# One VectorE pass for mask and row maximum, and steps that a planner may put on either of two engines

## The chip, the cores and the metric

The kernel runs on one core of a Trainium2 chip. The metric is the device time of one execution in microseconds (us). A core has TensorE (PE: matmuls, and PEld for the loading of their weights), VectorE (DVE), ScalarE (ACT), GpSimd (POOL) and SyncE (SP, which issues most transfers here). Matmul results go to PSUM, which has eight banks of 128 x 512 f32; DVE and ACT read PSUM in this kernel, POOL doesn't.

## What is computed

16 examples of 256 rows with 128 features pass six residual blocks, all in f32. Cut to what matters:

```python
x = x + 0.5 * L0_ffn(layernorm(x))     # gated: silu * linear, two hidden 512x512 layers with gelu
x = x + L0_attn(layernorm(x))          # non-local attention without a softmax
x = x + 0.5 * L0_ffn(layernorm(x))
x = x + 0.5 * L1_ffn(layernorm(x))     # top-2 of 8 low-rank experts, chosen by the first row
x = x + L1_attn(layernorm(x))          # 16 heads of 8, rotary positions, causal
x = x + 0.5 * L1_ffn(layernorm(x))
# inside L1_attn:
scores = jnp.einsum('bhqd,bhkd->bhqk', q, k) * scale
scores = jnp.where(causal, scores, -jnp.inf)
out = jnp.einsum('bhqk,bhkd->bhqd', softmax(scores, axis=-1), v)
```

## The kernel before, in words

The examples are worked in nine groups: seven of two examples (512 rows, "wide") and two of one (256 rows, "narrow"). Each group passes a first feed-forward with the non-local attention behind it, and a second feed-forward with experts, attention and experts behind it. x stays in SBUF throughout.

**The order is planned while the program is written.** Each piece of work is a generator whose steps (`step`, line 228) name an engine, an assumed duration in us, what they need, and the buffers and PSUM banks that they take or drop. A loop at the end of `macaron_kernel` keeps an assumed clock for each engine, asks `begin` (927) when each waiting step could start, and lets `issue` (975) write the earliest. Within an engine that order is the program's; at run time the engines only wait for data. `dve`, `act` and `pool` (237 to 243) give the durations. `find` (914) hands out PSUM banks: the attention's scores take banks 0 to 3 together, and a step with one bank may borrow one of those if `LOAN` us of waiting are saved. The feed-forwards are the main line, with all other lines fitted in. When the main line has ended, `awake` (962) issues products of the identity (`ident` times `ident`) into expected gaps of PE, 0.7 of each gap; the text calls them fillers.

**Feed-forward** (`ffn`, 329): w1T and w2T products, `silu` on ACT, the product on DVE, then two hidden layers in which seven block products replace eight. `sums` (360) makes for each layer four differences T of blocks of h, the first on DVE, the other three on POOL. `left` (384) copies one product to h on ACT. The w3s products end the feed-forward.

**Layernorm** (`normed`, 265): bn_stats and bn_aggr on DVE; four small operations on POOL give rstd and shift; then one ACT operation per 128 rows writes xn. `by_feature` (280) transposes xn on PE and copies it from PSUM to xnT on DVE.

**Attention** (`attention`, 652): `rotary` (633) makes keys and queries, with a last addition on POOL; `keys` (678) writes four masked copies of the keys, on ACT; `queries` (688) two of the queries (qz), on DVE. `maxima` (711) computes scores once to find each row's maximum: for each half t of an example's rows, PE writes scores of 4 x 2 heads x w keys (w is 256 for t=1, 128 for t=0), DVE adds the causal mask `causal` to the diagonal part in PSUM, and one reduction gives the negated maxima of eight heads, into tile mx. `queries_with` (747) transposes mx and adds it to the queries by `mrow`, so that the scores which `weighted` (767) computes again have their maximum subtracted already. There ACT takes the exponential (pr), POOL zeroes the upper triangle, PE multiplies by the values. In the last two groups (`late`) maxima goes by halves of the heads.

The core of the maxima, for each t and each list of pairs:

```python
for n in range(len(pairs)):
    yield dve(8 * P)
    d = sc[:, :, 2 * n : 2 * n + 2, t * P : w]
    nc.vector.tensor_tensor(d, d, causal...to_broadcast([P, 4, 2, P]), ALU.add)
...
for n, v in enumerate(pairs):
    yield dve(8 * w, drop=...)
    nc.vector.tensor_reduce(to[:, :, 1 - v], sc[:, :, 2 * n : 2 * n + 2, :], AX.X, ALU.max, negate=True)
```

All engine instructions go through a helper at line 220, so that the profile shows nearly every one as L220; they are told apart by engine, operation and tile. The tile pb is the whole of PSUM.

Of the kernel before, what the change touches and what calls it, by code (L numbers as in the profile page):

```python
# [12 lines left out]
F32 = mybir.dt.float32  # L13
# [6 lines left out]
P = 128  # L20
# [6 lines left out]
LANDING = 2.2  # L27
LOAN = 2.0
PATIENCE = 2.0
# [20 lines left out]
NEG = -1e30  # L50
# [4 lines left out]
def macaron_kernel(ctx: ExitStack, tc: tile.TileContext, a: dict, out: bass.AP):  # L55
# [63 lines left out]

    causal = cst.tile([P, P], F32, name="causal")  # L120
    ones = cst.tile([1, P], F32, name="ones")
    pht = cst.tile([P, D], F32, name="pht")
# [69 lines left out]
    def constants():  # L192

        yield step("POOL", 1.4, needs=(("in", 0, 0),))
        nc.gpsimd.memset(causal, 0.0)
        nc.gpsimd.affine_select(
            out=causal, in_=causal, compare_op=ALU.is_ge, fill=NEG, base=0, pattern=[[-1, P]], channel_multiplier=1
        )
        nc.gpsimd.memset(ones, 1.0)
        yield step(None, 0.0, sets=(("constants",),))  # L200

        for b in store_of["vm"]:
            yield step("POOL", 1.8)
            nc.gpsimd.memset(b.t, 0.0)
            yield step("POOL", 0.6, drop=(b,))
            for j in range(4):
                o = 8 + 16 * (j // 2)
                nc.gpsimd.memset(b.t.rearrange("p t r j c -> p (t r) j c")[:, :, j, o : o + DK], 1.0)
        for b in store_of["mx"]:
            yield step("POOL", 0.3, drop=(b,))  # L210
            nc.gpsimd.memset(b.t, 0.0)
# [15 lines left out]

    def step(engine, us, table=None, banks=0, take=(), drop=(), after=None, needs=(), sets=(), tiles=None, lag=0.0):
        return dict(
            engine=engine, us=us, table=table, banks=banks, take=take, drop=drop, after=after, needs=needs, sets=sets, lag=lag,  # L230
            tiles=tiles,
        )

    def pe(us, **kw):
# [30 lines left out]
    def normed(t0, n, needs=()):  # L265
        yield step("DVE", 0.12 + 0.26 * n, needs=needs)
        st = sml.tile([P, GT, 6], F32, name="st")
        for t in range(n):
            nc.vector.bn_stats(st[:, t, :], x[:, t0 + t, :])
        mv = scales(st, n)  # L270
        yield step("POOL", 1.2 + 0.17 * n)
        rstd, shift = inverse(mv, n)
        (xn,) = yield step("ACT", 0.39 * n, take=("xn",))
        for t in range(n):
            nc.scalar.activation(
                xn.t[:, t, :], x[:, t0 + t, :], AF.Identity, bias=shift[:, t : t + 1], scale=rstd[:, t : t + 1]
            )
        return xn

    def by_feature(n, xn, keep=False):  # L280
        pt, xnT = yield pe(0.11 * n, banks=1, take=("xnT",), drop=() if keep else (xn,))
        v = pt.t.rearrange("p (t n) -> p t n", n=P)
        for t in range(n):
            nc.tensor.transpose(v[:, t, :], xn.t[:, t, :], ident)
        yield dve(n * P, drop=(pt,))
        nc.vector.tensor_copy(xnT.t[:, : n * P], pt.t[:, : n * P])
        return xnT
# [41 lines left out]
    def ffn(which, t0, n):  # L329
# [30 lines left out]
        def sums(l, h, T):  # L360

            for i, e, x, y, needs in (
                (1, "DVE", (0, 1), (0, 0), ()),
                (2, "POOL", (1, 1), 1, ()),
                (3, "POOL", (1, 1), (0, 1), ()),
                (4, "POOL", (1, 0), 2, (("P6", l, me),)),
            ):
                needs += tuple(k for b in (x, y) if type(b) is tuple for k in has(l, *b))
                made = (("T", i, l, me),)
                drop = (T[2],) if i == 4 else ()  # L370
                (T[i],) = yield (
                    dve(N, needs=needs, take=("T",), sets=made, drop=drop) if e == "DVE"
                    else step("POOL", 0.05 + 0.002 * N, needs=needs, take=("T",), sets=made, drop=drop)
                )
                engine = nc.vector if e == "DVE" else nc.gpsimd
                engine.tensor_tensor(
                    T[i].t[:, :, :M], block(h, *x), T[y].t[:, :, :M] if type(y) is int else block(h, *y), ALU.subtract
                )
# [5 lines left out]
        def left(l, a, nh):  # L384

            yield act(N, sets=(("P1", l, me),))
            nc.scalar.copy(block(nh, 1, 1), in_two(a))

# [110 lines left out]
    def nonlocal_attn(t0, n):  # L499
# [4 lines left out]
        def product(us, lhs, rhs, name, drop=()):  # L504
# [3 lines left out]
            for b in range(nb):  # L508
# [4 lines left out]
                else:  # L513
                    nc.tensor.matmul(pp[:, b, :], lhs[:, b, :], rhs, start=True, stop=True)
            yield dve(nb * D, drop=(bk,))
            m = sml.tile([P, 2, D], F32, name=name, bufs=1)
            nc.vector.tensor_copy(m[:, :nb], pp[:, :nb])
            return m
# [74 lines left out]
    def experts(sg):  # L593
        xn = yield from normed(sg.t0, sg.n, (("ffn", 0, (1, sg.t0)), ("ffn", 1, (1, sg.t0)), ("constants",)))
        xnT = yield from by_feature(sg.n, xn)
        if sg.first:
            nb = len(sg.parts)
            yield step("POOL", 0.2 + 0.1 * nb)
            cls = sml.tile([P, 2, P], F32, name="cls", bufs=2)
            nc.gpsimd.tensor_copy(  # L600
                cls[:, :nb],
                xnT.t[:, : sg.n * P].rearrange("p (b s) -> p b s", b=nb)[:, :, 0:1].to_broadcast([P, nb, P]),
            )
            merged["before", sg.g] = yield from gated(nb, cls)
            yield step(None, 0.0, sets=(("before", sg.g),))
        yield from applied(("before", sg.g), sg, xnT)

    def gated_ahead(g, nb, y):
# [15 lines left out]
        for b in range(nb):  # L624
            nc.tensor.matmul(pc[:, b, :], y[:, b, :], ones, start=True, stop=True)
        yield dve(nb * D, drop=(bk,))
        cls = sml.tile([P, 2, P], F32, name="cls", bufs=2)
        nc.vector.tensor_copy(cls[:, :nb], pc[:, :nb])
        merged["after", g] = yield from gated(nb, cls)
# [3 lines left out]
    def rotary(c0, N, xnT, n, rot):  # L633
# [12 lines left out]
        nc.vector.stream_shuffle(rot[:, 1, :N], rot[:, 1, :N], [i ^ 1 for i in range(32)])  # L646
        yield pool(N)
        nc.gpsimd.tensor_tensor(rot[:, 0, :N], rot[:, 0, :N], rot[:, 1, :N], ALU.add)

    kept = {}  # L650

    def attention(sg):
# [25 lines left out]
        def keys():  # L678
# [3 lines left out]
            for j in (0, 2, 1, 3):  # L682
                yield step("ACT", 0.28 + 0.00083 * N, sets=(("km", sg.t0, j),) + ((("kept", g),) if j == 3 and sg.first else ()))
                nc.scalar.activation(
                    km[:, PLANE[j], c0 : c0 + N], kT[:, :N], AF.Identity, bias=kone[:, j : j + 1], scale=kmask[:, j : j + 1]
                )

        def queries():
# [3 lines left out]
            for v in range(2):  # L692
                yield step("DVE", 0.15 + 0.0005 * N, sets=(("qz", sg.t0, v),))
                nc.vector.tensor_scalar(qz[:, v, c0 : c0 + N], qT[:, :N], qmask[:, v : v + 1], None, ALU.mult)
            yield step(None, 0.0, needs=(("km", sg.t0, 3),), drop=(rot,))
# [7 lines left out]
        v0 = sg.parts[0][1][0]  # L703
        yield step("ACT", 0.53 + 0.225 * n, drop=(bk,), sets=(("v", sg.t0),))
        for i in range(2):
            nc.scalar.copy(
                vm.t[:, v0 : v0 + n].rearrange("p t r (i h) c -> p (t r) i h c", i=2)[:, :, i, :, 16 * i : 16 * i + DK],
# [3 lines left out]
        def maxima(i):  # L711
# [5 lines left out]
            def scores(t, pairs):  # L717
# [16 lines left out]
                sc = q.t[:, :, : len(pairs) * 2 * w].rearrange("p r (j k) -> p r j k", k=w)  # L734
                for n in range(len(pairs)):
                    yield dve(8 * P)
                    d = sc[:, :, 2 * n : 2 * n + 2, t * P : w]
                    nc.vector.tensor_tensor(
                        d, d, causal.unsqueeze(1).unsqueeze(1).to_broadcast([P, 4, 2, P]), ALU.add
                    )  # L740

                to = mx[0].t[:, t, :].rearrange("p (r o h c) -> p r h o c", r=4, o=2, h=2)[:, :, :, :, 0]
                for n, v in enumerate(pairs):
                    yield dve(8 * w, drop=(q,) if n == len(pairs) - 1 else ())
                    nc.vector.tensor_reduce(to[:, :, 1 - v], sc[:, :, 2 * n : 2 * n + 2, :], AX.X, ALU.max, negate=True)

# [167 lines left out]
    def find(n, short):  # L914
# [10 lines left out]
        return best.clear, [best], None  # L925

    def begin(line):

# [10 lines left out]
        if n["table"] == "exp" and table[0] != "exp" and not ended[0]:  # L939
            t += PATIENCE  # L940
        return max(t, clock[n["engine"]]) if n["engine"] else t

# [32 lines left out]
    def issue(line):  # L975
# [5 lines left out]
        t = max([t, since] + [s.clear for s in bufs])  # L981
        e, us = n["engine"], n["us"]
        if e:
# [84 lines left out]
def _tables():  # L1068
# [15 lines left out]
    sel = np.stack([RANK * ~second, RANK * second, f % RANK, np.where(second, -0.5, 0.5)], axis=1)  # L1084
    made = {"cosT": cos, "sinT": sin, "qmask": qmask, "kmask": kmask, "kone": kone, "mrow": mrow, "sel": sel}
    return {n: np.ascontiguousarray(v, dtype=np.float32) for n, v in made.items()}
# [55 lines left out]
```

## Time and profile before

| | |
|---|---|
| median of 3 runs | 973.13 us (972.97 to 973.29) |
| profiled execution | 972.04 us |
| its span, first to last instruction | 970.4 us |
| mean granted TensorE clock | 0.996 |
| ACT table loads | 78 |
| DMA | 13.76 MB, mean 14 GB/s |

The span is that of the profiled execution alone, and 1.6 us of its time lie around it. Busy time is the time in which an engine had an instruction under way; instructions that overlap on one engine are not counted twice, so a group's busy time can be less than its count times the mean. In a group's line stand: source line, engine, operation, tile written <- tiles read, shapes, count | busy us, mean ns of one | idle us of the engine just before, and what ended it. A wait's line gives us in total, times, and the longest. The chain of work that ended last goes back from the last instruction, at each step to what released it.

### The profile page before, as it was taken

Reading aid. Unit: us, or ns where it says so; the run is one execution under the profiler, and the core shown is the slowest. Engines: PE = TensorE matmul, PEld = TensorE weight load, DVE = VectorE, ACT = ScalarE, POOL = GpSimd, SP = SyncE. Lnnn points to the kernel's source line nnn. Section 1 sums busy time; section 2 is a strip of 40 time slices with the busy share of each in tenths; the row PEclk is TensorE's granted clock in tenths of the full one; section 3 lists DMA queues with packets and bytes.
Section 4 is the critical chain, followed back from the end, with each engine's and each line's share of the span. In section 5 each row is a group of like instructions: output and inputs, shape, how many; then the busy total and the mean of one; then the engine's idle time right before and its main releaser. Section 6 shows DMA issues by size and latency. Waiting matters only on the chain.

```text
span 970.4 us, 16624 instructions
## 1 busy us (share of the span) xinstructions
PE 918.1 (95%) x6600; PEld 690.0 (71%) x6600; DVE 646.1 (67%) x1470; ACT 450.2 (46%) x672; POOL 371.8 (38%) x572
## 2 busy tenths in 40 slices
PE   6999999999999999999999999999999899898887
PEld 4877878666676767686786667767777777786565
DVE  5654456937687646857569376856577676869673
ACT  2244344365535463553552755254652547472342
POOL 5422334241534225341553425242444135343342
PEclk9999999999999999999999999999999999999999
DMA  7000000000000000000000000000000000000000
GB/s 249 16 1 1 1 12 7 5 1 2 12 23 1 1 1 22 12 1 1 13 22 1 2 12 1 23 1 1 12 12 11 1 12 2 23 7 12 1 22 7
DMA packets 14717, 13.76 MB, mean 14 GB/s; under 512 B 2032, under 2 KB 12080, under 8 KB 14640
## 3 DMA queue, kind: packets, MB, share of 16 engines
q1 hardware_dynamic: 12624, 8.11, 2.8%
q0 software_dynamic: 1600, 4.20, 1.5%
q8 instruction: 52, 0.85, 0.4%
q10 hardware_dynamic: 416, 0.39, 0.1%
q14 instruction: 25, 0.20, 0.1%
HBM read 10.60 MB, written 2.10 MB: 13 GB/s over the span
## 4 chain that ended last, share of the span: by engine, by line
PE 65%; DVE 18%; ACT 7%; issue 4%; POOL 3%; DMA 1%; SPq 1%; DVEq 0%; ACTq 0%; POOLq 0%
PE pb L220 65%; DVE mx L220 4%; DVE h L220 3%; ACT pr L220 3%; DVE pb L220 2%; ACT L220 2%; ACT xn L220 1%; POOL rstd L220 1%; DVE st L220 1%; DVE x L220 1%; DMA w3s<-in_w3T_dram 1%; DVE T L220 1%; ACT sil L220 1%; DVE den L220 1%; DVE gw L220 1%
## 5 line engine op out<-in xcount | busy, mean ns | idle before, releaser
L220 DVE TENSOR_TENSOR h<-h,pb 128x512 f32<-128x512 f32 (+1 forms) x180 | 111.9, 622 | 104.4 <-PE pb L220 98.7
L220 PE MATMUL pb<-T,hS 128*128 128x256 f32 (+1 forms) x576 | 134.5, 366 | 10.7 <-DVE h L220 5.8
L220 ACT ACTIVATE h<-h 128x512 f32<-128x512 f32 (+1 forms) x108 | 62.4, 581 | 173.7 <-DVE h L220 173.6
L220 POOL TENSOR_TENSOR T<-h,T 128x512 f32<-128x512 f32 (+1 forms) x72 | 83.7, 1163 | 122.5 <-DVE T L220 56.8
L220 PE MATMUL pb<-qkv 32*128 32x256 f32 (+2 forms) x1536 | 115.1, 405 | 14.9 <-ACT pr L220 7.6
L220 POOL TENSOR_SCALAR nm<-mv 128x4 f32<-128x4 f32 (+3 forms) x62 | 15.1, 243 | 274.1 <-DVE mv L220 267.4
L220 PEld LDWEIGHTS pb<-T,hS 128*128 128x128 f32 x576 | 95.0, 190 | 33.4 <-issue 8.1
L220 ACT ACTIVATE pr<-pb 128x1536 f32<-128x1536 f32 x64 | 92.4, 1449 | 54.6 <-PE pb L220 47.2
L220 ACT ACT_TABLE_LOAD x77 | 98.8, 1283 | 39.2 <-PE pb L220 36.3
L220 POOL TENSOR_SCALAR_AFFINE_SELECT pr<-pr 128x512 f32<-128x512 f32 x128 | 78.2, 635 | 100.0 <-ACT pr L220 99.7
L220 ACT ACTIVATE xn<-x,shift,rstd 128x128 f32<-128x128 f32 x188 | 77.7, 483 | 79.3 <-POOL shift L220 73.6
L220 DVE TENSOR_REDUCE mx<-pb 128x8 f32<-128x2048 f32 (+1 forms) x64 | 111.8, 1750 | 0.5
L220 DVE TENSOR_TENSOR pb<-pb,causal 128x1024 f32<-128x1024 f32 x64 | 78.5, 1227 | 36.1 <-PE pb L220 33.6
L220 PEld LDWEIGHTS pb<-qkv 32*128 32x128 f32 x1536 | 68.2, 184 | 48.1 <-ACT pr L220 16.0
L220 PE MATMUL pb<-xnT,w1T 128*128 128x512 f32 (+1 forms) x144 | 69.0, 561 | 3.0 <-ACT sil L220 1.5
L220 PE MATMUL pb<-xnT,w2T 128*128 128x512 f32 (+1 forms) x144 | 68.7, 559 | 1.3 <-ACT sil L220 1.0
L220 DVE SCALAR_TENSOR_TENSOR h<-pb,s,sil 128x512 f32<-128x512 f32 (+1 forms) x72 | 48.2, 684 | 31.1 <-ACT sil L220 21.2
L220 PE MATMUL pb<-T,h2T 128*128 128x256 f32 (+1 forms) x288 | 64.8, 362 | 3.3 <-DVE T L220 3.0
L220 PE MATMUL pb<-T,h1T 128*128 128x256 f32 (+1 forms) x288 | 66.3, 360 | 0.6 <-DVE T L220 0.6
L220 DVE TENSOR_TENSOR x<-x,pb 128x256 f32<-128x256 f32 (+2 forms) x79 | 37.4, 474 | 43.0 <-PE pb L220 42.8
L220 PE MATMUL pb<-h,h1T 128*128 128x256 f32 (+1 forms) x288 | 65.3, 364 | 0.2 <-DVE h L220 0.2
L220 PE MATMUL pb<-h,hS 128*128 128x256 f32 (+1 forms) x288 | 65.4, 360 | 0.0
(121 smaller groups left out, 1558.3 us busy)
## 6 DMA issues: line engine op xcount, KB each, us to landing
out_dram<-x SPq DMA_DIRECT2D x7, 256.0 KB, 2.3
x<-in_x_dram SPq DMA_DIRECT2D x6, 256.0 KB, 4.7
h1T<-in_h1T_dram SPq DMA_DIRECT2D x1, 1024.0 KB, 9.3
h2T<-in_h2T_dram SPq DMA_DIRECT2D x1, 1024.0 KB, 10.1
ab<-in_eab_dram,at POOLq DMA_INDIRECT x32, 2.8
x<-in_x_dram SPq DMA_DIRECT2D x3, 128.0 KB, 4.9
w1T<-in_w1T_dram SPq DMA_DIRECT2D x1, 256.0 KB, 3.9
w2T<-in_w2T_dram ACTq DMA_DIRECT2D x1, 256.0 KB, 4.1
```

Source lines behind the costliest of these rows:

```text
L220: return lambda *args, **kw: tc.keep_in_program_order(getattr(self.engine, name)(*args, **kw))
```

## The change

The mask and the row maximum become one DVE operation per head and t: it adds a 128 x w piece of `causal` (now 256 wide, with the diagonal in its right half) to the scores in PSUM and at the same time keeps the maximum in an accumulator, which is written to one column of mx. The maximum isn't negated any more; the table `mrow` is. The step of each two heads becomes two steps of four operations.

`either` makes a step with two possible engines, each with an assumed duration. `pick`, called from `begin` and `issue`, takes the engine whose clock, duration and hop to the next engine would end first. `either` is used for xn (ACT or DVE), the copies xnT, gram, gph, eff, cls and h (DVE or ACT), all four T and rotary's addition (DVE or POOL), one copy for the experts' choice (POOL or DVE), the keys' and queries' masked copies and the copy of the values (ACT or DVE). `LOAN` becomes 1.0. The tile `ones` shrinks to one element that is broadcast.

```diff
-LOAN = 2.0
+LOAN = 1.0
+SPARED = 0.0
...
+    def either(*alt, **kw):
+
+        return step(alt[0][0], alt[0][1], alt=alt, **kw)
...
+    def copied(n, **kw):
+
+        return either(("DVE", 0.07 + 0.00105 * n), ("ACT", 0.16 + 0.00083 * n), **kw)
...
-        (xn,) = yield step("ACT", 0.39 * n, take=("xn",))
+        (xn,) = yield either(("ACT", 0.39 * n), ("DVE", 0.21 * n), take=("xn",))
...
-                (T[i],) = yield (
-                    dve(N, needs=needs, take=("T",), sets=made, drop=drop) if e == "DVE"
-                    else step("POOL", 0.05 + 0.002 * N, needs=needs, take=("T",), sets=made, drop=drop)
+                (T[i],) = yield either(
+                    ("DVE", 0.07 + 0.00105 * N), ("POOL", 0.19 + 0.0021 * N), needs=needs, take=("T",), sets=made, drop=drop
...
-                for n in range(len(pairs)):
-                    yield dve(8 * P)
-                    d = sc[:, :, 2 * n : 2 * n + 2, t * P : w]
-                    nc.vector.tensor_tensor(
-                        d, d, causal.unsqueeze(1).unsqueeze(1).to_broadcast([P, 4, 2, P]), ALU.add
-                    )
...
-                    yield dve(8 * w, drop=(q,) if n == len(pairs) - 1 else ())
-                    nc.vector.tensor_reduce(to[:, :, 1 - v], sc[:, :, 2 * n : 2 * n + 2, :], AX.X, ALU.max, negate=True)
+                    for h in range(2):
+                        yield step("DVE", 4 * (0.1 + 0.00105 * w), drop=(q,) if n == len(pairs) - 1 and h else ())
+                        for r in range(4):
+                            d = sc[:, r, 2 * n + h, :]
+                            nc.vector.tensor_tensor_reduce(
+                                out=d, in0=d, in1=causal[:, 2 * P - w :], scale=1.0, scalar=-3e38, op0=ALU.add, op1=ALU.max,
+                                accum_out=to[:, r, 1 - v, h, 0:1],
+                            )
...
+    def pick(n, t):
+
+        if n["alt"]:
+            n["engine"], n["us"] = min(n["alt"], key=lambda a: max(t, clock[a[0]]) + a[1] + HOP[a[0]] + (SPARED if a[0] == "DVE" else 0.0))
...
-    made = {"cosT": cos, "sinT": sin, "qmask": qmask, "kmask": kmask, "kone": kone, "mrow": mrow, "sel": sel}
+    made = {"cosT": cos, "sinT": sin, "qmask": qmask, "kmask": kmask, "kone": kone, "mrow": -1.0 * mrow, "sel": sel}
```

## The prediction

> **What bounds the kernel now.** I read the page from the top: busy shares, the chain, the costliest groups. Then the waits of TensorE alone, and the busy time by stage.
>
> ```profile
> span 970.4 us, 16624 instructions
> PE 918.1 (95%) x6600; PEld 690.0 (71%) x6600; DVE 646.1 (67%) x1470; ACT 450.2 (46%) x672; POOL 371.8 (38%) x572
> ...
> PE 65%; DVE 18%; ACT 7%; issue 4%; POOL 3%; DMA 1%; SPq 1%; DVEq 0%; ACTq 0%; POOLq 0%
> PE pb L220 65%; DVE mx L220 4%; DVE h L220 3%; ACT pr L220 3%; DVE pb L220 2%; ACT L220 2%; ACT xn L220 1%; POOL rstd L220 1%; DVE st L220 1%; DVE x L220 1%; DMA w3s<-in_w3T_dram 1%; DVE T L220 1%; ACT sil L220 1%; DVE den L220 1%; DVE gw L220 1%
> ```
>
> TensorE is full. The chain's largest item off it is the mask and maximum: mx 4% and pb 2%, some 58 us. By stage (each row: stretch, its length, then busy time of PE, PEld, DVE, ACT, POOL):
>
> ```profile
> 0.00:871.00 871.00, 836.70 (x5729) 629.37 (x5729) 577.50 (x1319) 417.35 (x628) 339.06 (x508) 1.00 0.05 15
> 871.00:971.00 100.00, 81.40 (x873) 60.61 (x871) 68.63 (x151) 32.83 (x45) 32.70 (x64) 0.99 0.04 10
> ```
>
> 871 is where the last feed-forward's w3s products end. Up to there TensorE idles 34.3 us: 8.1 in the first 50, 26.2 after. The last 100 us (the tail) hold 18.6 us of idleness, and 116 fillers, `ident` products that `awake` issues into expected idleness. 13 fillers took 3.17 us in the timeline, 0.244 each, so 28 us of the tail's busy time is no work: 47 of its 100 us are waiting. Between 50 and 870 TensorE waited thus:
>
> ```profile
> PE pb L220 <- DVE h L220: 6.4, 9, 1.5
> PE pb L220 <- DVE T L220: 3.6, 6, 0.9
> PE pb L220 <- ACT sil L220: 3.4, 4, 1.0
> PE pb L220 <- DVE mx L220: 3.4, 6, 0.9
> PE pb L220 <- ACT pr L220: 2.8, 7, 1.1
> PE pb L220 <- POOL T L220: 2.2, 4, 0.9
> ```
>
> So the middle has at most 26 us to give, the tail 47. The matmuls stay the same, fillers apart.
>
> **Part 1: the mask and the maximum.** Now (64 adds, 32 + 32 reductions):
>
> ```profile
> L220 DVE TENSOR_TENSOR pb<-pb,causal 128x1024 f32<-128x1024 f32 x64 | 78.5, 1227 | 36.1 <-PE pb L220 33.6 <-ACT h L220 2.1
> L220 DVE TENSOR_REDUCE mx<-pb 128x8 f32<-128x2048 f32 x32 | 73.1, 2284 | 0.4
> L220 DVE TENSOR_REDUCE mx<-pb 128x8 f32<-128x1024 f32 x32 | 38.7, 1216 | 0.1
> ```
>
> Together 190.3 us of DVE. Instead there are 512 fused passes, half 128 wide, half 256, and the built program shows a second instruction behind each, writing one column of mx: 1024 for 128. The arithmetic per pair of heads falls from 1024 added and 2048 reduced elements to 2048 (t=1), from 1024 and 1024 to 1024 (t=0); the fixed costs rise eightfold. No row shows a fused pass or its read, so bounds. Low: four BATCH_NORM_STATS2 of 128 elements took 0.87 us, one 0.279, so followers come 0.197 apart, 64 ns over 128 elements at the reductions' 1.04 ns (2284-1216 over 1024); passes at 0.197 and 0.330 with the read hidden make 256 x 0.527 = 135 us. High: the full durations of x<-x,pb (0.286 at 128, 0.416 at 256) and a read as long as wt<-mx (0.154): 256 x 1.010 = 259 us. I take the low passes and a read of 0.092, the MATCH_VALUE_LOAD row, since it too is an instruction without a tensor pass in front of which nothing waits: 256 x (0.289 + 0.422) = 182 us, 8 below now. On the chain 58 us x (182/190.3 - 1) = -2.5 us; at the ends -17 and +21.
>
> [...]
>
> **Part 2: steps on either of two engines.** The built order shows that the choice is made. By instructions:
> - xn: 142 of 188 go from ACT (77.7/188 = 0.413 each, -58.7) to DVE (1.12 us for four, 0.28, +39.8). Four in a row take 1.12 instead of 1.65, which the chain meets about six times: 6 x 0.53 x 142/188 = -2.4 us.
> - The differences T: 59 wide and 15 narrow ones from POOL (1.285, 0.73) to DVE (0.684, 0.41): DVE +46.6, POOL -86.8. TensorE's 2.2 us behind POOL T should go: -2.2.
> - rot: 8 + 3 from POOL to DVE, +6.7. Copies of h, vm and keys' masks to DVE: 18, 16, 10, +10.7, about +6, +4.8. cls to DVE +2.
> - To ACT: 28 xnT, 21 of gram, gph, eff and cls, 10 qz: DVE -17.8, -8.2, -5.3; ACT +15.2, +7.2, +7.1. ACT also gets 19 more table loads (97 for 78), 19 x 1.283 = +24.4.
>
> Sums: DVE +85 (with the mask 723, 75% of the span), ACT -25, POOL -101. The table loads I cost at nothing: the moved xn hide them, 58.7 against 24.4. Without that cover: the chain holds 2% (19 us) of table loads out of 98.8, so 24.4 x 0.2 = +4.9. The indirect DMAs' number is the same; on POOL's queue less stands in front of them.
>
> What DVE's load costs: between 50 and 870 TensorE waited for DVE 16.4 us (h, T, mx, and 2.0, 0.6, 0.4 for x, y, xnT) at a DVE share of 66%. If waits go with the inverse of the idle share, 0.34/0.25, that is +5.9. Since a step goes to DVE only where its clock is expected to be free first, I take half, +3.
>
> Added work with two SBUF inputs also meets POOL. At 25.05 us (columns: start, length, operation):
>
> ```profile
> 24.61 1.64 POOL L220 TENSOR_TENSOR T<-h,T 128x512 f32<-128x512 f32 x1 [1.03 <-DVE T L220]
> 26.22 1.71 POOL L220 TENSOR_TENSOR T<-h 128x512 f32<-128x512 f32 x1
> ```
> ```profile
> 25.05 3.43 DVE L220 TENSOR_TENSOR h2T<-h2T,rot 128x512 f32<-128x512 f32 x2
> ```
>
> DVE took 1.75 instead of 0.68 each, POOL 1.64 and 1.71 instead of 1.27. With 85 such T and rot on DVE and POOL busy 28% of the time, 24 meetings x 1.07 = 25 us on DVE, of which 18% (DVE's share of the chain) would be 4.6; the +3 contains what I take of it. [...]
>
> **Part 3: the tail.** LOAN 1.0 and the choices let the planner finish more attention before the last w3s. In the built order, behind that point, transposes of mx fall from 10 to 8 and softmax exponentials from 14 to 11: one example's maxima are out of the tail. In the chain these stood at 877.7 to 893.9, 16.2 us; but some 8 us of matmuls (24 pr, 40 qkv, 4 wo and small ones) come in front of the point instead. -8 net. Fillers give the same from another side: 25 fewer (91 for 116), 25 x 0.244 = 6.1, and as fillers fill 0.7 of an expected gap, 8.7 us less gap. I take -8.7.
>
> **Sum.** -2.5 - 2.4 - 2.2 + 0 + 3 - 8.7 = -12.8. The profiled execution took 972.04 (span 970.4 and 1.6 around it): 959.2. The runs' median, 973.13, is 1.1 higher: **960**, -1.3%.
>
> **Rivals.**
> - *Larger gain* (0.22). The read hides behind the next pass and DVE's relief reaches the middle. For it: followers only 64 ns over their elements. Mask at 135 us: -17 instead of -2.5, so 946; with the +3 gone 943.
> - *DVE full* (slower, 0.20). Passes don't overlap because each read must wait until its pass has drained: 259 us, in the maxima's own steps. DVE then reaches (646+85+69)/970 = 82%; waits for DVE go as 0.34/0.18: 16.4 x 0.89 = +14.6. Chain: +21 - 2.4 - 2.2 + 14.6 - 8.7 = +22: 995. It decides from where a pass of 256 with its read costs over about 0.48 us (0.422 x 207/182; with 207 us in all the chain gains 5 and the waits 8, against -13 from the other terms). For it: 1024 instructions, a planner that counts 0.369 for that pair; against it: BN rows that overlap.
> - *Eaten in the middle* (0.10). The gains stand, 15.8, but table loads (+4.9), meetings with POOL (+4.6) and DVE's load in full (+5.9) take them: -0.4, so 971 to 975.
> - That the choice isn't made is excluded by the built order.
>
> **Chances.** The forecast's case (953 to 969) 0.48. A measurement of this kernel tells about 0.2%, 1.9 us, from no change. The third rival lies across that bound and is split 0.02, 0.06, 0.02. Faster by more: 0.48 + 0.22 + 0.02 = 0.72; within: 0.06; slower: 0.02 + 0.20 = 0.22. The range, 944 to 981, leaves out the far ends of both rivals.
>
> **What will show it.** The pair: fused passes of 256 plus read, spaced 0.42 (0.33 or 0.57 by the ends). The tail after the last w3s near 82 us instead of 100 with 8 more of matmuls before it. PE waits for POOL T gone, for DVE h and mx at most a third up. DVE busy about 723. If TensorE's idle time between 50 and 870 rises beyond 35 us, the sum is wrong in Part 2; if the tail is as long as now, in Part 3; if DVE's mask rows exceed 207 us, in Part 1.

## The result, and the profile after

The change makes no difference that can be measured: 972.66 us (median of 12 runs, 969.52 to 975.53) against 973.05 (12 runs, 971.73 to 973.84), a ratio of 0.9997 [0.9981, 1.0012] (in brackets a 95% interval, here and below). The runs of the changed kernel spread over 6.0 us and those of before over 2.1; the profiled one took 970.75 at a mean granted clock of 0.988, while the five above 973.5 had 0.981 to 0.984. The forecast was 960 and a clear gain. The time came out where the third rival, "eaten in the middle", had put it, but not by that rival's way: the middle gained. The page of the changed kernel, at the places that were shown of before (span, busy times, chain by engine and by line):

```profile
span 969.0 us, 17385 instructions
PE 924.9 (95%) x6550; PEld 696.2 (72%) x6550; DVE 714.0 (74%) x2584; ACT 428.9 (44%) x564; POOL 282.0 (29%) x481
...
PE 76%; DVE 13%; ACT 5%; issue 3%; SPq 1%; POOL 1%; DMA 0%; POOLq 0%; DVEq 0%; ACTq 0%
PE pb L221 76%; DVE pb L221 4%; ACT L221 2%; ACT pr L221 2%; DVE xn L221 1%; DVE h L221 1%; DVE mx L221 1%; DVE rot L221 1%; DVE T L221 1%; ACT h L221 1%; POOL pr L221 1%; SPq L74 1%; DVE qkv L221 0%; ACT sil L221 0%; DVE den L221 0%
```

Two things are to be seen. The chain did what was hoped: TensorE's share of it rose from 65 to 76%, and mx and pb fell from 6 to 5%. And TensorE idles less (44.1 us of the span instead of 52.3), but it is *busy* 6.8 us longer, although 50 products are gone, 25 fillers of two, worth 6.1 us. The same work thus took 12.9 us longer. The mean granted clock is 0.988 instead of 0.996, and 0.8% of 969 us is 8 us, an estimate of what the clock can account for of the 12.9, and about what the shorter waits gave (8.2). It is rather too high, since part of the lower clock lies in the start (0.91 there instead of 0.97), where TensorE was busy for 43.3 us instead of 43.1.

The stages show where. Each is bounded by ends of w3s products, the last of a feed-forward, found in the timeline of either profile (length in us, with TensorE's idle time behind the stroke):

| stage | before | after | difference |
|---|---|---|---|
| start, to the first group's w3s | 51.2 / 8.1 | 57.0 / 13.7 | +5.8 |
| middle, to the 12th feed-forward's | 577.3 / 14.8 | 570.1 / 5.1 | -7.2 |
| to the 17th's | 214.7 / 9.9 | 219.0 / 9.5 | +4.3 |
| last feed-forward | 27.9 / 1.5 | 47.5 / 5.0 | +19.6 |
| tail | 99.3 / 18.0 | 75.4 / 10.8 | -23.9 |

**The start.** The timeline of after (start, length, engine and operation; in brackets the idle time before and who ended it):

```profile
16.53 1.26 POOL L221 TENSOR_TENSOR h1T<-h1T,rot 128x512 f32<-128x512 f32 x1
16.61 6.66 DVE L221 TENSOR_SCALAR xn<-x,rstd,shift 128x128 f32<-128x128 f32 x4 [1.18 <-POOL shift L221]
17.73 1.80 POOL L221 MEMSET vm<- 128x2048 f32 x1
19.50 1.30 POOL L221 TENSOR_TENSOR h1T<-h1T,rot 128x512 f32<-128x512 f32 x1
20.74 3.12 POOL L221 MEMSET vm<- 128x128 f32 x9
```

The second group's four xn, chosen for DVE, take 6.66 us instead of 1.12, as four at 75.12 do with nothing of POOL's beside them; POOL is never free in this stretch, and its own operations keep the lengths that they had before: 1.26 and 1.30 for these two products (1.26 both), 1.80 for the memset of 128x2048 (1.80). TensorE waited for it up to 7.2 us at a time. Before, ACT wrote them in 1.65 beside the same POOL work:

```profile
15.90 1.65 ACT L220 ACTIVATE xn<-x,shift,rstd 128x128 f32<-128x128 f32 x4 [5.54 <-DMA rot<-in_woT_dram]
```

The waits of TensorE over the whole span of after (us, times, longest):

```profile
PE pb L221 <- DVE xn L221: 13.4, 9, 7.2
PE pb L221 <- ACT pr L221: 8.2, 11, 1.7
PE pb L221 <- DVE mx L221: 3.6, 4, 1.4
```

**The end.** The last feed-forward as a whole, first of before, then of after (columns as in the prediction; the third number from the end is the granted clock):

```profile
843.20:871.10 27.90, 26.36 (x254) 22.71 (x254) 18.14 (x46) 18.10 (x28) 10.81 (x20) 1.00 0.02 6
```
```profile
846.10:893.60 47.50, 42.54 (x382) 33.57 (x381) 33.46 (x142) 28.16 (x35) 12.77 (x25) 0.89 0.03 7
```

128 more products, 16.2 us more of busy TensorE and 3.4 more of idleness. The busy time by stretch, two of after, then two of before:

```profile
870.00:880.00 10.00, 7.74 (x47) 5.20 (x40) 9.92 (x58) 0.90 (x3) 1.20 (x4) 0.67 0.00 0
880.00:890.00 10.00, 8.39 (x64) 7.32 (x67) 7.51 (x28) 6.36 (x9) 1.19 (x2) 0.82 0.06 15
```
```profile
870.00:880.00 10.00, 9.75 (x100) 6.72 (x98) 7.13 (x22) 7.62 (x11) 6.60 (x16) 1.00 0.01 2
880.00:890.00 10.00, 7.77 (x73) 6.38 (x72) 9.82 (x20) 1.39 (x5) 1.10 (x1) 1.00 0.05 14
```

In after the last feed-forward is still under way in these 20 us (in before the tail has begun). DVE is busy throughout the first ten, ACT and POOL hardly at all; TensorE idles 2.3 of them, and the granted clock is 0.67 on the mean. Taken finer, it is 1.00 up to 873.37 and then one half for 10.24 us:

```profile
873.37:883.61 10.24, 9.19 (x37) 6.78 (x32) 9.99 (x55) 3.01 (x6) 2.20 (x5) 0.50 0.00 0
```

If half of these 9.19 busy us is due to the clock, that is 4.6 of the 19.6, an estimate. TensorE's timeline of after says how it comes about:

```profile
872.02 3.04 PE L221 MATMUL pb<-qkv 32*128 32x256 f32 x16 [1.30 <-DVE mx L221]
...
878.73 0.76 PE L221 MATMUL pb<-ones,y 1*128 1x128 f32 x2 [0.60 <-DVE x L221]
```

Scores of the next maxima wait for DVE's passes, TensorE's queue stands behind them, and after the wait these 16 products take 3.04 us, the first six of them in pairs 0.38 apart and still at full clock. In the middle of the profile of before such 16 mostly took 0.94.

The kernel before has such a stretch too, the second of its two above: DVE as full, TensorE idle for 2.2 us. But this is in the tail, where fillers run in the gaps, and the clock stays at 1.00:

```profile
882.46 3.17 PE L220 MATMUL pb<-ident 128*128 128x128 f32 x26
```

Up to the end of the main line `awake` issues no filler. That the fillers are what kept the clock up is argued and not shown: no run put any in front of that point, and the tail of `shake_choice` (section 4 of the experiments) had 0.93 on the mean with them.

**The fused pass itself** kept what was forecast. Timeline of after:

```profile
869.38 0.43 DVE L221 CUSTOM_DVE_ANT_0 pb<-pb,causal 128x256 f32<-128x256 f32 x1 [0.80 <-PE pb L221]
869.73 0.14 DVE L221 DVE_READ_ACCUMULATOR2_ANT mx<- 128x1 f32 x1
869.73 0.47 DVE L221 CUSTOM_DVE_ANT_0 pb<-pb,causal 128x256 f32<-128x256 f32 x1
870.11 0.14 DVE L221 DVE_READ_ACCUMULATOR2_ANT mx<- 128x1 f32 x1
...
870.87 0.14 DVE L221 DVE_READ_ACCUMULATOR2_ANT mx<- 128x1 f32 x1
870.87 0.71 DVE L221 STREAM_TRANSPOSE den<-pb 128x512 f32<-128x512 f32 x1
```

A pass of 0.47 and a read of 0.14 repeat every 0.38, not every 0.61: the rows overlap. So a cost taken from the groups' means would be far off. Four of 256 take 1.63 us in all (869.38 to 871.01), four of 128 take 1.09 (877.20 to 878.29): 64 x 2.72 = 174 us for the whole part, where 182 were forecast and 190.3 were there before. The next operation of DVE starts together with the last read, 1.49 us after the first pass (0.96 for four of 128, at 878.16).

### The profile page after: what moved, and what is told of

It reads as the page before. It is cut to its first block, busy times and chain, and to the rows that moved or that the text cites. A ratio compares the mean times of both kernels' runs of the same rounds, so it can differ in the third digit from the quotient of the medians.

```text
span 969.0 us, 17385 instructions
## 1 busy us (share of the span) xinstructions
PE 924.9 (95%) x6550; PEld 696.2 (72%) x6550; DVE 714.0 (74%) x2584; ACT 428.9 (44%) x564; POOL 282.0 (29%) x481
## 4 chain that ended last, share of the span: by engine, by line
PE 76%; DVE 13%; ACT 5%; issue 3%; SPq 1%; POOL 1%; DMA 0%; POOLq 0%; DVEq 0%; ACTq 0%
PE pb L221 76%; DVE pb L221 4%; ACT L221 2%; ACT pr L221 2%; DVE xn L221 1%; DVE h L221 1%; DVE mx L221 1%; DVE rot L221 1%; DVE T L221 1%; ACT h L221 1%; POOL pr L221 1%; SPq L74 1%; DVE qkv L221 0%; ACT sil L221 0%; DVE den L221 0%
## 5 line engine op out<-in xcount | busy, mean ns | idle before, releaser
L221 DVE CUSTOM_DVE_ANT_0 pb<-pb,causal 128x128 f32<-128x128 f32 (+1 forms) x512 | 165.9, 388 | 23.7 <-PE pb L221 23.4
L221 POOL TENSOR_SCALAR_AFFINE_SELECT pr<-pr 128x512 f32<-128x512 f32 x128 | 81.8, 663 | 202.6 <-ACT pr L221 202.5
L221 PE MATMUL pb<-qkv 32*128 32x256 f32 (+2 forms) x1536 | 126.6, 407 | 11.8 <-ACT pr L221 8.2
L221 PEld LDWEIGHTS pb<-T,hS 128*128 128x128 f32 x576 | 98.0, 194 | 24.3 <-issue 8.0
L221 POOL TENSOR_SCALAR nm<-mv 128x4 f32<-128x4 f32 (+3 forms) x62 | 17.6, 285 | 316.2 <-DVE mv L221 314.3
L221 PEld LDWEIGHTS pb<-qkv 32*128 32x128 f32 x1536 | 76.1, 184 | 45.6 <-ACT pr L221 20.3
L221 DVE DVE_READ_ACCUMULATOR2_ANT mx<- 128x1 f32 x512 | 71.7, 140 | 0.0
L221 PE MATMUL pb<-h,h2T 128*128 128x256 f32 (+1 forms) x288 | 65.0, 361 | 0.0
L221 PEld LDWEIGHTS pb<-w3s,h 128*128 128x128 f32 x512 | 60.8, 192 | 4.5 <-issue 2.5
L221 DVE TENSOR_SCALAR xn<-x,rstd,shift 128x128 f32<-128x128 f32 x142 | 52.6, 458 | 15.6 <-POOL shift L221 15.1
```

What stands on the lines that cost most here:

```text
L221: return lambda *args, **kw: tc.keep_in_program_order(getattr(self.engine, name)(*args, **kw))
```

## The experiments

Theories, by the letters that the expectations use. **G**: the middle's gain is given back at the start, where four xn on DVE meet POOL's work, and in the last feed-forward. **P**: fused passes are too dear, as in the rival "DVE full". **Q**: the planner counts fused passes too short (4 x (0.1 + 0.00105 w): 1.48 and 0.94 us, against 1.63 and 1.09 from first start to last end), and so TensorE's queue stands behind waits that the plan doesn't know. **H**: the splitting of a step into halves lets other work in between. **S**: the order that the planner happens on is worth several us either way, whatever the rules. **C**: only steps on either engine make the order depend so much on small differences, so that Part 2's effect is that of an order and not of the engines' relief. All times are medians; the ratio is to the kernel before, in the same session.

**1. One part at a time.** Part 1 alone in the kernel before (`fused_only`):

```diff
-                for n in range(len(pairs)):
-                    yield dve(8 * P)
...
-                    nc.vector.tensor_reduce(to[:, :, 1 - v], sc[:, :, 2 * n : 2 * n + 2, :], AX.X, ALU.max, negate=True)
+                    for h in range(2):
+                        yield step("DVE", 4 * (0.1 + 0.00105 * w), ...)
+                        for r in range(4):
...
+                            nc.vector.tensor_tensor_reduce(
```

> The kernel before with Part 1 alone: fused pass and accumulator read in steps of four, every step on its old engine, LOAN 2.0. Theory G: in the changed kernel four passes of 256 with their reads take 1.63 us, four of 128 about 1.07, so 64 x 2.70 = 173 us against 190 of adds and reductions: same or a little faster, 967 to 973. Theory P: their rows sum to 237.6 us, 47 more than now, and with 58 us of mask and maximum on the chain the time rises by 10 or more, to 983 or above.

969.31 us, 0.9964 [0.9951, 0.9978]. DVE is busy 625.3 us, 20.8 less than before: the passes are cheaper than what they replace, and P falls.

The other half (`choice_only`): the changed kernel with the old add and reduction, and so with `either`, `pick` and LOAN 1.0 alone.

> The changed kernel with Part 1 undone: adds and reductions as before (without the negation, with mrow's sign as changed), their old assumed durations, all choices kept; the planner makes its order anew. Theory G: DVE loses a little, the start and the end remain as in the changed kernel: 972 to 980. Theory P: without the passes' cost the choices show their gain: 958 to 966.

961.55 us, 0.9876 [0.9861, 0.9892]. The start is as bad (xn 6.65 us at 16.28, first w3s end 56.8), and still this half alone is 1.2% faster. Two gains, of 3.7 and 11.5, that together give 0.4: either the parts hurt each other, or each number is partly that of an order. (961.55 is within what P expected of this run, but P had fallen with the run before.)

**2. The start.** The four xn back on ACT, everything else, the plan too, as it was (`xn1_on_act`), or POOL's memsets of vm later (`late_memsets`):

```diff
+        if not normeds:
+            chosen[0] = "ACT"
+        normeds.append(t0)
```
```diff
-            yield step("POOL", 1.8)
+            yield step("POOL", 1.8, needs=(("ffn", 1, (0, 4)),))
```

> The changed kernel with one decision undone by hand: the second group's first xn (four operations) is written on ACT instead of DVE, and the planned order is kept, so nothing else moves. Theory G (the gain of the middle is given back at the start and in the last feed-forward): in the changed kernel these four operations took 6.66 us on DVE while POOL ran its memsets and weight products, and PE came 5.8 us later out of the first group than before; on ACT they take 1.65 us, so the time falls by 5 to 6, to about 967, and the first group's w3s products end near 51.2 as before. Theory P (the fused passes cost too much, and the start is caught up later): the time falls by less than 2, to 971 or more.

969.02 us, 0.9959 [0.9945, 0.9972]. The first w3s end at 52.9 instead of 57.0; a wait for ACT's xn of 4.6 is left, as there was before. 4.1 of the 5.8 us return at the start, and 3.6 of the whole time, where 5 to 6 were expected. TensorE's rows in the profile come in the same order as in the changed kernel, so nothing but these four operations is moved.

> The changed kernel, with POOL's memsets of the two vm tiles held back until the second group's first feed-forward has ended; the planner's order changes from there on. If POOL's work at the same time is what stretched the four xn operations on DVE from 1.1 to 6.66 us, they take 2.5 us or less here (one weight product of POOL still beside them), and the first group's w3s end near 52.5 instead of 57.0; the time falls by some 4, with a few us either way from the new order. If DVE's xn is slow for another reason at that place, they still take over 5 us.

967.42 us, 0.9941 [0.9926, 0.9956]; first w3s end 52.7. The timeline:

```profile
15.82 2.48 POOL L221 TENSOR_TENSOR h1T<-h1T,rot 128x512 f32<-128x512 f32 x2
15.91 3.00 DVE L221 TENSOR_SCALAR xn<-x,rstd,shift 128x128 f32<-128x128 f32 x4 [1.17 <-POOL shift L221]
```

With 2.48 us of POOL's work beside them the four take 3.00, more than expected, since both products now fell beside them. With 7.5 us beside them they took 6.66. G is shown for the start. The single records of the two traces say what holds xn: here the first two each end 0.08 us after one of the products (1.26 and 1.30 long), and the other two, with nothing beside them, take 0.34; in the changed kernel the first and the third end 0.08 us after a memset of 1.80 that followed the product (3.00 and 3.60 long). Both kinds of POOL's work hold them. The later memsets move other work too, so the rest of this gain isn't charged to the start.

**3. The plan's costs and its steps.** Measured costs (`true_costs`), and eight passes in one step at measured cost (`whole_steps`):

```diff
-                        yield step("DVE", 4 * (0.1 + 0.00105 * w), ...)
+                        yield step("DVE", 4 * (0.1325 + 0.00105 * w), ...)
```
```diff
+                    yield step("DVE", 8 * (0.1325 + 0.00105 * w), ...)
                     for h in range(2):
-                        yield step("DVE", 4 * (0.1 + 0.00105 * w), ...)
```

> The changed kernel with the fused steps planned at what they were measured: 1.605 us for four passes of 256 (1.63 measured) and 1.07 for four of 128, instead of 1.475 and 0.938. Theory Q (the planner counts DVE's new steps too short, 64 x 0.26 = 17 us in all, so it fills DVE too far and its order is late at the end): the time falls to 958 to 965, and the last feed-forward no longer takes 47 us. Theory S (the two parts don't disturb each other; the order that the planner happens on is worth several us either way, above all near the end, and the changed kernel met a poor one): any value between 960 and 977, with no tie to the cost.

962.85 us, 0.9902 [0.989, 0.9915]. But the last feed-forward, which Q was to explain, is still 48.7 us long at a clock of 0.89; the gain lies between it and the start (782.8 us instead of 789.1), with 8.2 us of idleness instead of 14.6. The rows of the fused pass speak against Q's ground as well: DVE goes on to its next operation 1.49 and 0.96 us after the first of four passes, which is what the planner counted before (1.48 and 0.94). So this run's costs are too long for the time in which DVE is taken, and its gain isn't explained by truer costs.

> The changed kernel with the fused passes of a pair in one planned step of eight again, at the measured cost (3.21 and 2.14 us), so that nothing is planned between its halves. Theory H (steps cut in halves let other DVE work in between, so that each maximum and the work between both finish later): 958 to 965, and faster than the kernel with halves at the measured cost. Theory Q: like that kernel within 3 us. Theory S: no tie.

969.32 us, 0.9963 [0.995, 0.9976]: 6.5 us slower than halves at the same costs. H finds no support; by C, below, one order is a weak test of it.

Measured costs and the xn on ACT (`true_xn1`):

> The changed kernel with both mends: fused steps planned at their measured length (962.9 alone) and the second group's first xn on ACT with the order kept (3.7 off the changed kernel alone). The order is that of the kernel with the measured lengths, so the start's gain should add to it: 958 to 960. If the later waits take the start's gain up, 962 to 963.

960.26 us, 0.9874 [0.9858, 0.989], 2.6 below `true_costs`, with TensorE's rows in the same order; first w3s end 52.4, the rest of the stages as there to within 0.5 us. The start's cost thus shows a second time in another order.

**4. Other orders of the same kernels.** `SLACK` (line 31; 30 before) is a tie window of the planner: among steps of one engine that could start within it, rank decides. It touches neither what is computed nor any engine's choice by itself.

```diff
-SLACK = 0.05
+SLACK = 0.06
```

0.04, 0.06 and 0.07 were tried, as `shake2_`, `shake_` and `shake3_`, of the kernel before, of Part 1 alone (fused), of the choices alone (choice) and of both (after).

> The changed kernel with the planner's tie window SLACK at 0.06 instead of 0.05: no step's cost or engine rule changes, but the order comes out anew. Theory Q: within 3 us of the changed kernel, 970 to 976, since the costs are still too short. Theory S: it may move by 5 us or more.

> The kernel with the choices and the old adds and reductions (choice_only, 961.55), with SLACK at 0.06 instead of 0.05. Theory Q: within 3 us, 958 to 965. Theory S: it may move by 5 us or more.

> The kernel before with SLACK 0.06 instead of 0.05. Theory S (the order that the planner happens on is worth several us, whatever the rules): it moves by 3 us or more either way. Theory C (only the choice of engines makes the planner so sensitive, because it multiplies the decisions that hang on small differences of the assumed clocks): within 3 us, 970 to 976.

> The kernel before with Part 1 alone (969.3 at SLACK 0.05), at 0.06. Theory S: it moves by 3 us or more. Theory C: within 3 us, 966 to 972. If Part 1 is a gain of its own, it is faster than the kernel before at the same 0.06, by 2 to 6.

> The choices with the old adds and reductions, at SLACK 0.04 (961.6 at 0.05, 980.1 at 0.06). Theory S and theory C both: anywhere between 958 and 982. A value near 962 makes 980 the odd one, a value near 975 makes 962 the lucky one.

> The kernel before at SLACK 0.04 (973.1 at 0.05, 973.6 at 0.06). Theory C (without choices the order is steady): 970 to 976. Theory S: may lie elsewhere.

> Part 1 alone at SLACK 0.04 (969.3 at 0.05, 959.5 at 0.06). If Part 1 by itself is worth the 21 us of DVE that it saves, spread by where it is on the chain, its mean over the three lies 5 to 12 below that of the kernel before: 958 to 972 here. If 959.5 was a lucky order, 968 or more.

> The changed kernel at SLACK 0.04 (972.7 at 0.05, 967.0 at 0.06). If Part 2's choices are worth nothing on the mean once Part 1 is there, its mean over the three lies at or above that of Part 1 alone: 965 to 978 here. If they are worth 5 or more, 950 to 960.

> Part 1 alone at SLACK 0.07, a fourth order of the same rules: 957 to 971 if the mean gain of Part 1 is 5 to 12; 972 or more if the gain was the orders' luck.

> The choices with the old adds and reductions at SLACK 0.07 (971.1 at 0.04, 961.6 at 0.05, 980.1 at 0.06; mean 970.9). If Part 2 is worth little on the mean: anywhere from 960 to 982, the mean of four 968 to 974.

> The changed kernel at SLACK 0.07, a fourth order with both parts. If the choices cost what the start loses (4) and gain about that in the middle, the mean of four lies within 4 of that of Part 1 alone; this one 960 to 976.

Measured, in us (the column 0.05 is from above; ratios of the others below):

| | 0.04 | 0.05 | 0.06 | 0.07 | mean |
|---|---|---|---|---|---|
| before | 972.64 | 973.05 | 973.62 | | 973.1 |
| Part 1 alone | 960.20 | 969.31 | 959.48 | 959.45 | 962.1 |
| choices alone, with LOAN 1.0 | 971.14 | 961.55 | 980.07 | 987.25 | 975.0 |
| both | 969.26 | 972.66 | 966.97 | 979.09 | 972.0 |

Ratios to before: Part 1 alone 0.9871 [0.9854, 0.9887], 0.9867 [0.985, 0.9883], 0.986 [0.9843, 0.9876]; choices alone 0.999 [0.9979, 1.0001], 1.0081 [1.0068, 1.0094], 1.0155 [1.0138, 1.0172]; both 0.9966 [0.9953, 0.9978], 0.9936 [0.9923, 0.9949], 1.006 [1.0042, 1.0078]; before itself 1.0001 [0.9991, 1.001] and 1.0006 [0.9996, 1.0015].

C is shown for choices put into the kernel before: the same windows move that kernel by 1 us, and the choices alone by 26. It isn't shown on top of Part 1, where both parts move by 12 and Part 1 alone by 10. S falls for the kernel before, which it had moving by 3 us or more. Line by line, TensorE's rows in the profiles differ thus from those at 0.05: the kernel before in 7 and 131 lines, Part 1 alone in some 300, at 0.04 and 0.06 only after the first 789 of 1122 rows. With choices they differ from row 120 or so of some 1090 on, in 343 to 837 lines. The likely reason, argued and not shown: a step that goes to the other engine moves two assumed clocks, and with them every later choice. The 1.2% gain of `choice_only` was that of one order. What C doesn't cover: Part 1 alone, for which it had 966 to 972 at 0.06 (959.48 measured), also spreads by 10, since its order at 0.05 is worse behind the 14th feed-forward than the other three (which lie within 0.8 us). The end of the program is sensitive without choices too. Expectations were missed by choices alone at 0.07 (up to 982 expected), by both at 0.07 (up to 976), and by the mean of both, which was to lie within 4 of that of Part 1 alone and lies 9.9 above it.

By stages, means of the profiled executions of those kernels (us):

| | start | middle | to the 17th | last feed-forward + tail | span |
|---|---|---|---|---|---|
| before (3) | 51.5 | 577.3 | 215.0 | 127.4 | 971.2 |
| Part 1 alone (4) | 51.9 | 567.3 | 222.4 | 118.6 | 960.3 |
| choices alone (4) | 56.3 | 571.7 | 220.4 | 123.9 | 972.4 |
| both (4) | 56.1 | 571.7 | 217.4 | 124.8 | 970.0 |

Part 1 gives 10 in the middle and 9 at the end and costs 7 in between. Part of that is work which crossed the bounds: 24 products fewer run in its middle, and 40 to 66 more up to the 17th. Its middle is 567.2 to 567.4 in all four, but these are hardly different orders up to there, so this is one observation rather than four. Choices on top of it cost 4 at the start, 4 in the middle and 6 at the end, and give 5 between. The start's loss (3.7 to 6.0 us against the mean of before) is in all eight kernels with choices. The slowest kernel, choices alone at 0.07, shows the end of after once more, and worse (its last feed-forward ends at 904.9):

```profile
880.00:890.00 10.00, 6.41 (x33) 4.49 (x33) 9.47 (x17) 0.76 (x2) 1.28 (x5) 0.60 0.00 0
890.00:900.00 10.00, 9.43 (x54) 8.53 (x54) 6.51 (x26) 4.58 (x7) 1.77 (x2) 0.54 0.05 15
900.00:910.00 10.00, 8.55 (x111) 6.32 (x109) 2.84 (x10) 7.69 (x8) 4.92 (x10) 1.00 0.01 2
```

DVE is full for 10 us, TensorE idles 3.6 of them, and in the next 10, when it is 94% busy, the clock granted is still 0.54: 54 products in 9.43 us, where 111, not all of the same shapes, take 8.55 afterwards. The clock is at one half from 882.04 to 899.11. This mechanism needs no fused passes: here the old add and reduction run. The mean clock of this kernel is 0.976. It doesn't come with every order: three of the eight kernels with choices have no time at half clock in their last feed-forward.

## Why the prediction was wrong

*Part 1, the passes' cost: right in size, and slightly high.* 182 us forecast, 174 from first start to last end of its steps, 169.5 by DVE's total in Part 1 alone (190.3 - 20.8). The forecast spacing of a pair of 256 was 0.42; it is 0.38, and 0.25 for 128 instead of 0.29. A pass with its read takes about 115 ns more than its elements at the 1.04 ns that the prediction used for one (0.38 - 256 x 0.00104 = 0.114; 0.25 - 128 x 0.00104 = 0.117). The trace has rows of 455 ns for a pass of 256, the read's of 140 not counted, with a spacing of 380, read included; as a price of instructions in a row the rows' own lengths are too high here. "DVE full" falls, on its own condition: 0.38 is below 0.48.

*Part 1, "On the chain 58 us x (182/190.3 - 1) = -2.5 us": mis-sized.* Part 1 alone measured -12.4, -3.7, -14.1 and (against the mean of before) -13.6 in four orders. The ratio scaled the rows of the chain and left out that a DVE relieved of 21 us can come earlier to everything else; the rival of a larger gain, whose term was -17, had that effect in it.

*Part 2, -2.4 - 2.2 + 3: wrong in sign.* The counts were right: DVE 714 (723 forecast), ACT 429 (425), POOL 282 (271). TensorE's waits for POOL's T are gone, as forecast (2.2 us before, none after). In the middle waits fell more than forecast: idleness 14.8 to 5.1, although DVE's load rose, so "+3" was too dear there. It was too cheap at the start: "a step goes to DVE only where its clock is expected to be free first" is true of an assumed clock that knows nothing of POOL's work beside it, and 5.5 us were lost in one place. The prediction priced these meetings for T and rot, operations with two SBUF inputs, and not for xn. It had 25 us on DVE for the first; the wide T there took only some 6 more than at 0.684 each (45 at 0.782, 42 at 0.729). The 142 xn took 52.6 us, where 39.8 were counted. Of the stretched xn two each ended 0.08 us after an instruction of POOL's, beside products (`late_memsets`, 1.26 and 1.30 long) and beside memsets (the changed kernel, 1.80) alike; by what the one engine holds the other no run shows.

*Part 3, "some 8 us of matmuls … come in front of the point instead. -8 net": the step that failed.* The tail became 75.4, even shorter than the 82 forecast, and fillers fell to 91 as forecast. But in front of the point it cost 19.6 us in the last feed-forward and 4.3 before it, not 8: these sum to 23.9, all that the tail gave. The moved work was counted in matmuls at full clock on a TensorE that has nothing to wait for. It came with its maxima, on a DVE that then had no free time for 10 us, in a stage where no filler runs; TensorE waited, and the half clock granted after the wait made its own products longer (the eight `pb<-wo,oT` at 876.05 took 2.08 us; 1.10 in the kernel before at 888.33, at 1.00). That this jam is the reason is read from the profile; no run took the maxima out of that stage in the same order. Over four orders the last feed-forward and the tail together changed by -2.6 (124.8 - 127.4), where the prediction had -8.7 for LOAN and the choices; Part 1 alone changed them by -8.8, and LOAN and the choices on top of it cost 6.

*And the sum as such.* It added terms as if the order were given. With choices it isn't: spreads of 12 and 26 us among equal kernels are as large as the forecast gain, and a range that treats one built order's terms as the change's worth can't be trusted to better than that. The prediction's condition on idleness between 50 and 870, 35 us, wasn't met (it fell to 15.6); the condition on the tail wasn't either. Both looked at stages one by one and missed that work had crossed the point between them.

*What stays open.* Whether longer assumed costs (Q) help on the mean or gave one good order: two kernels share that order. How much of the choices' loss is LOAN 1.0 was not tried. The means of three or four orders are rough: choices alone, +1.9, can't be told from nothing, whereas choices on top of Part 1 lost in all four orders (+9.1, +3.4, +7.5, +19.6), a mean of 9.9.

Versions that beat both kernels: Part 1 alone at a window of 0.06 or 0.07, 959.48 and 959.45 us, and both parts with measured costs and the first xn on ACT, 960.26 us.

## What to carry over

When a planner orders the program, a change's gain is not one number until it has been measured in several orders: shake a tie window, first on the kernel before, and distrust any gain that is smaller than what shaking does. Work that is moved from behind a point to in front of it must be priced with everything that it brings to each engine there, with the waits that this makes, and at the clock that is granted there (0.89 on the mean in the last feed-forward of the changed kernel, 1.00 in that of before). And an engine choice by assumed clocks has to know of work on another engine that stretches its own (four xn on DVE took 6.66 us beside POOL's, 1.12 with nothing beside them), or it will choose the engine that is free and then held.

## What was not expected of the hardware

- Four xn of 128x128 on DVE, out of SBUF into SBUF: 1.12 us alone, 3.00 beside two of POOL's products, 6.66 beside products and memsets; one of them took 3.60 instead of 0.34.
- A fused pass with its accumulator read: rows of 0.455 and 0.140 us (means), a spacing of 0.38.
- The granted clock fell to one half for 10.24 us (changed kernel) and for 17.07 us (choices alone at 0.07), though TensorE was busy for 9.19 and 14.41 us of these; in the second, it was 94% busy in one 10 us at 0.54.
